# Order and engines of the head in a two-layer kernel of styled convolutions and feed-forward products

## The chip, the core and the metric

The kernel runs on one core of a Trainium2 chip. The core has TensorE (matrix products; PE in the profile, its weight loads PEld), VectorE (DVE), ScalarE (ACT), GpSimd (POOL) and SyncE (SP); each takes its instructions in the order in which they stand in its own queue, and waits for the others by semaphores. DMAs are issued from SP, ACT and POOL. The metric is the device time of one execution in microseconds (us).

## The reference, cut to what matters

Two layers run one after the other on x of 32 x 64 x 1024. Each is a chain of four small convolutions over 64 channels, scaled per sample by a style, and behind it a feed-forward product over the 1024 positions; the result is added to x. The head of the kernel is about the first part:

```python
def _layer(x, style, w, b, mw, mb, typ):
    s = style @ mw.T + mb
    weight = SCALE * w * s[:, None, :, None]
    demod = lax.rsqrt(jnp.sum(weight * weight, axis=(2, 3)) + EPS)
    weight = weight * demod[:, :, None, None]
    ...  # 'same', 'upsample' + blur, 'same', blur + 'downsample'; each + bias
x = x + _L0_ffn_ref(_L0_cond_ref(x, cond_512, ...), A, B, Wr)
x = x + _L1_ffn_ref(_L1_cond_ref(x, cond_512, ...), qweight, scales, zeros, bias)
```

The first feed-forward product picks 16 of 64 experts of rank 16 for each row; the second has weights of four bits.

## The kernel before, in words

All samples are worked on in 16 pairs: two samples' 64 channels fill the 128 partitions. The four convolutions are linear, so all but the first are composed into one set of filters per pair. For pair p of layer i:

- `load_x` (L523) fetches the samples into two buffers, `xdv(n % 2)`. A buffer is free again once `differences` (L538) has read it.
- `differences` scales by the style and forms three tiles (`xe`): one on ACT (L541), two on VectorE (L542, L543). `first` (L548) makes three products `c` with the matrix c0 (L554, L559) and adds bias and scale (ACT L556, VectorE L560 to L563).
- `composed1` (L460) makes the product `g` of w2t with scaled weights `r` (GpSimd L462), copied to `gs` by ACT (L476). `composed2` (L481) makes `f` from `gs` and the blurred weights w1b (18 passes on TensorE, L488), and copies it out (ACT L500, VectorE L501, GpSimd L503).
- `rest` (L566) applies the filters (`r`, L577), with ACT L590 and L585, GpSimd L586 and L587, VectorE L591. `outer` (L594) puts the four border columns in, which `ends` (L358) has computed apart; `turned` (L621) transposes the result for the feed-forward product (`h`, L662).

`factors` (L158) makes a layer's tables, in steps that a `yield` ends:

- step 1 issues the loads: mw (the style's weights), cwr, cur, biases; on SP and on ACT's queue;
- step 2 squares the weights (L192 to L195), spreads them into cw, cu, c0 and w3 (ACT L199, L203, L204; GpSimd L200), builds the blurred weights in six sums and two copies (GpSimd L213, L218), transposes the third convolution's weights into w2t (TensorE L223, ACT L224), multiplies the style (`sps`, L230), adds mb (L233), squares (L236), multiplies by the squared weights (`dps`, L239), takes root and reciprocal (ACT L247, VectorE L248);
- step 3 makes the scales `al` and biases `be` and their copies by pairs, alp, bep, styp (L256 to L275);
- step 4 carries the biases through the convolutions, two products `cs` (L282), each behind the other's result, to cst and cst2 (L284 to L286), which L590 reads.

`ends` works on the border columns of all pairs at once, in a chain: `ye` (L391), scaled; `ue` (L410), scaled; a blur; `ve` (L435), scaled; a blur; `re` (L446), scaled; copies into `re` (L455). "Scaled" is a product on VectorE (L371) and a sum on GpSimd (L372). A blur is two sums on GpSimd (L419, L420) and one instruction on VectorE (L421).

PSUM tiles come from three rings: mps has one bank (all of `sps`, `dps`, `cs`, `g`, `f`, `ye`, `ue`, `ve`, `re`, and w2t's transposes), cps three (`c`, `r`, transposes), fps four. A tile of a ring waits for the readers of the one whose bank it takes.

The order on each engine is made by a scheduling layer from the program's order and its own estimate of times; `tc.issue_after(v)` holds what is issued inside it behind instruction v in that order. It sets where an instruction stands in its queue and is no wait on the chip. `done` remembers such instructions by name.

The head of the main program, L898 to L930, runs step 1, loads pair 0, runs steps 2 and 3, begins pair 0 (`begin`: differences, first, composed1), runs step 4, loads pair 1, makes pair 0's filters (`weights(0)`), issues eight DMAs of the first product's weights from GpSimd (`load_a`, L304), begins pair 1, and interleaves `ends` with `rest` of pair 0. Behind it the main loop starts: `split_weights` (L290) divides each block of those weights into parts (VectorE L143, L299; ACT L298; GpSimd L297), held behind the last copy of `re`, `outer` and `turned`. The second layer's `factors` (set1, L977) runs a step at a time between pairs of the first layer's second product (`o`, L662, with transposes `ht`, L756), near 500 us.

Of the kernel before, what the change touches and what calls it, by code (L numbers as in the profile page):

```python
# [61 lines left out]
def adaln_ffn_kernel(ctx: ExitStack, tc: tile.TileContext, t, out: bass.AP):  # L62
# [95 lines left out]
    def factors(i, *rooms):  # L158
# [35 lines left out]
        for h in range(2):  # L194
            nc.vector.tensor_tensor(wsq[:, :, h], sq[:, :, 0], sq[:, :, 2], ALU.add)  # L195
# [5 lines left out]
        for h, hs in enumerate(halves):  # L201
            for e, o, k in (((0, 0, 0), (2, 0, 2), (2, 1, 1)), ((0, 0, 1), (0, 1, 0), (2, 1, 2)))[h]:
                nc.scalar.copy(c0[hs, e, halves[o]], cwr[hs, 0, k])  # L203
        nc.scalar.copy(w3, cwr[:, 3])  # L204


        t0 = tmp(NB + 1, C)
        t1 = tmp(NB + 1, C)
        nc.gpsimd.memset(t0.rearrange("p a b -> p (a b)"), 0.0)
        nc.gpsimd.memset(t1.rearrange("p a b -> p (a b)"), 0.0)  # L210
        nc.gpsimd.tensor_copy(t0[:, 1 : 1 + KT], cwr[:, 1])
        for n in range(KT + 1, NB + 1):
            nc.gpsimd.tensor_tensor(  # L213
                t1[:, 1 : 1 + n], t0[:, 1 : 1 + n], t0[:, 0:n], ALU.add
            )
            t0, t1 = t1, t0
        for hs in halves:
            done["blur"] = nc.gpsimd.tensor_copy(w1b[hs, :, hs], t0[hs, 1 : 1 + NB])  # L218


        ps = mpst(f"w2t{i}")
        for k in range(KT):
            nc.tensor.transpose(ps[:, k * P : (k + 1) * P], cw[:, 2, k], ident)  # L223
        nc.scalar.copy(w2t.rearrange("p a b -> p (a b)"), ps[:, : KT * P])  # L224
# [8 lines left out]
        nc.vector.tensor_tensor(sty, spv, mb.unsqueeze(2).to_broadcast([P, NL, B]), ALU.add)  # L233
        nc.vector.tensor_copy(sty0, sty[:, 0])

        nc.vector.tensor_tensor(sty2, sty, sty, ALU.mult)  # L236
        dpv = mpst(f"dps{i}")[:, : NL * B].rearrange("p (a b) -> p a b", b=B)
# [9 lines left out]
        nc.scalar.activation(dem, dpv, AF.Sqrt, bias=eps, scale=0.5)  # L247
        nc.vector.reciprocal(dem, dem)  # L248
# [109 lines left out]
    def ends(i, lo, hi, room, behind=None):  # L358
        n = hi - lo
        g = f"{i}_{lo}"  # L360
        used = [0]
# [6 lines left out]
        def scaled(dst, ps, l):  # L368
            a = alp[:, l, lo:hi].unsqueeze(2).to_broadcast([P, n, dst.shape[2]])
            b = bep[:, l, lo:hi].unsqueeze(2).to_broadcast([P, n, dst.shape[2]])  # L370
            nc.vector.tensor_tensor(dst, ps, a, ALU.mult)  # L371
            nc.gpsimd.tensor_tensor(dst, dst, b, ALU.add)  # L372
# [8 lines left out]
        with tc.issue_after(behind.ins) if behind else nullcontext():  # L381
            nc.vector.tensor_tensor(xe[:, :, 1:7], xg[:, lo:hi, 0, 0:6], s, ALU.mult)
            nc.vector.tensor_tensor(xe[:, :, 7:13], xg[:, lo:hi, 1, 2:8], s, ALU.mult)
# [32 lines left out]
        def blur(dst, v, count):  # L416

            m = sides(tmp(2 * count))
            nc.gpsimd.tensor_tensor(dst, v[..., 0:count], v[..., 3 : 3 + count], ALU.add)  # L419
            nc.gpsimd.tensor_tensor(m, v[..., 1 : 1 + count], v[..., 2 : 2 + count], ALU.add)  # L420
            nc.vector.scalar_tensor_tensor(dst, m, 3.0, dst, ALU.mult, ALU.add)  # L421
# [16 lines left out]
        scaled(ve[:, :, 2:14], ps, 2)  # L438
# [12 lines left out]
        scaled(rp, ps, 3)  # L451
# [96 lines left out]
    def first(i, n, xe):  # L548
# [8 lines left out]
        for q, w_, d in ((0, HQ, y[:, 0, :HQ]), (2, HQ - 1, y[:, 1, 1:HQ])):  # L557
            ps = cpst(f"c{i}_{n}_{q}")[:, :w_]
            nc.tensor.matmul(ps, c0[:, q], xe[:, q, :w_], start=True, stop=True)  # L559
            nc.vector.scalar_tensor_tensor(d, ps, a, yt[:, :w_], ALU.mult, ALU.add)  # L560
# [5 lines left out]
    def rest(i, n, y, f):  # L566
# [7 lines left out]
        for q, (m0, m1, n_) in enumerate(((0, 2, w_), (1, 3, HQ), (4, 5, w_))):  # L574
# [9 lines left out]
            if q == 1:  # L584
                nc.scalar.activation(m[:, q, :n_], ps, AF.Copy, scale=a)  # L585
                nc.gpsimd.tensor_tensor(u, m[:, 0, :w_], m[:, 1, :w_], ALU.add)  # L586
                nc.gpsimd.tensor_tensor(r[:, 1], m[:, 0, :w_], m[:, 1, 1:HQ], ALU.add)  # L587
            else:
                b = (cst if q == 0 else cst2)[:, n : n + 1]
                nc.scalar.activation(m[:, q, :n_], ps, AF.Identity, bias=b, scale=a)  # L590
        nc.vector.tensor_tensor(r[:, 0], m[:, 2, :w_], u, ALU.subtract)  # L591
# [320 lines left out]
    run(set0)  # L912
    first_done = done["xe"]
    load(1)
    weights(0)
    with tc.issue_after(done["sum"].ins):
# [162 lines left out]
```

## Time and profile before

Three runs gave 1017.24, 1017.95 and 1020.43 us, median 1017.95. One other execution was profiled: 1017.49 us, of which the span in the profile is 1015.4.

| | PE | PEld | DVE | ACT | POOL |
|---|---|---|---|---|---|
| busy us of the span | 953.8 | 841.4 | 634.7 | 368.6 | 466.9 |
| 0 to 25 us | 10.41 | 8.47 | 14.13 | 9.37 | 16.05 |
| 25 to 50 us | 18.52 | 15.17 | 13.45 | 8.79 | 13.83 |
| 50 to 75 us | 21.84 | 17.34 | 13.12 | 8.20 | 12.86 |
| 100 to 125 us | 24.08 | 17.63 | 9.57 | 9.14 | 10.83 |
| 175 to 200 us | 24.86 | 23.57 | 15.43 | 10.65 | 10.20 |

Busy time is the time with at least one instruction of the engine under way. Lines of the chain of waits give start, duration, engine, tile and source line; the chain is followed back from the last instruction, at each step to what released it. An fp32 product is recorded as two passes per instruction, so "x18" are nine products. PEclk is the TensorE clock that was granted, in tenths of full speed.

### The profile page before, as it was taken

To read this page: it belongs to the slowest core of one execution; us is meant where nothing else is said; L and a number is where in the kernel's file an instruction comes from. 1 tells how busy PE (TensorE), PEld (TensorE's weight loads), DVE (VectorE), ACT (ScalarE), POOL (GpSimd) and SP (SyncE) were. 2 spreads that over 40 slices of the span, in tenths; PEclk is the share of its full clock that TensorE was granted. 3 is DMA by queue.
4 is the path that set the end of the run, shared out by engine and by line. 5 is a ranking of instruction groups with operands and counts; after the bars stand their busy time and mean duration, and the time that the engine had idled before them with its cause. 6 is when DMAs were issued, how large, how long until landed. Compare 5 with 4: busy or idle time off the path is not lost.

```text
span 1015.4 us, 14211 instructions
## 1 busy us (share of the span) xinstructions
PE 953.8 (94%) x5046; PEld 841.4 (83%) x5046; DVE 634.7 (63%) x1275; ACT 368.6 (36%) x693; POOL 466.9 (46%) x638
## 2 busy tenths in 40 slices
PE   4788889999999999999989998999899999999997
PEld 3666679999999999994668887888898999899986
DVE  5557366666666666346974554486667766776654
ACT  3335344444444444323321111163334333433331
POOL 6557454443444334435762223226545555555544
PEclk9979989999999999999999999999999999999999
DMA  4631122222222221242353333352112221222111
GB/s 99 183 118 42 42 63 63 63 63 63 63 63 76 71 63 65 81 146 98 98 181 131 125 125 125 104 152 98 63 63 87 92 71 63 85 88 78 42 63 42
DMA packets 39894, 88.83 MB, mean 87 GB/s; under 512 B 12080, under 2 KB 20528, under 8 KB 39824
## 3 DMA queue, kind: packets, MB, share of 16 engines
q1 hardware_dynamic: 37616, 82.48, 25.9%
q0 software_dynamic: 1248, 4.46, 1.4%
q10 hardware_dynamic: 960, 0.99, 0.4%
q8 instruction: 40, 0.66, 0.3%
q14 instruction: 30, 0.25, 0.1%
HBM read 62.74 MB, written 25.17 MB: 87 GB/s over the span
## 4 chain that ended last, share of the span: by engine, by line
PE 74%; DVE 9%; POOL 6%; issue 5%; ACT 5%; DMA 1%; POOLq 0%; ACTq 0%; DVEq 0%; SPq 0%
PE h L662 17%; PE r L577 15%; PE o L662 13%; PE q L840 11%; PE f L488 8%; PE c L559 5%; DVE h L143 2%; PE c L554 2%; ACT yt L556 1%; ACT thx L604 1%; POOL wa L297 1%; PE ht L756 1%; DVE cv L563 1%; DVE sc L854 1%; DVE hs L684 1%
## 5 line engine op out<-in xcount | busy, mean ns | idle before, releaser
L577 PE MATMUL r<-cv 128*128 128x256 f32 (+1 forms) x768 | 181.6, 383 | 5.1 <-ACT rt L590 4.6
L577 PEld LDWEIGHTS r<-cv 128*128 128x128 f32 x768 | 143.2, 190 | 28.2 <-ACT rt L590 5.8
L590 ACT ACTIVATE rt<-r,cst,al 128x256 f32<-128x256 f32 x128 | 72.4, 565 | 164.2 <-PE r L577 151.8
L591 DVE TENSOR_TENSOR rs<-rt,ru 128x256 f32<-128x256 f32 x64 | 43.0, 672 | 103.4 <-ACT rt L590 55.5
L488 PEld LDWEIGHTS f<-gs,w1b 128*128 128x128 f32 x576 | 90.5, 200 | 3.8 <-ACT gs L476 1.1
L488 PE MATMUL f<-gs,w1b 128*128 128x192 f32 (+1 forms) x576 | 91.5, 315 | 1.2 <-ACT gs L476 0.6
L503 POOL TENSOR_TENSOR cv<-cv 128x256 f32<-128x256 f32 x64 | 48.0, 751 | 82.0 <-DVE cv L501 71.8
L501 DVE COPY cv<-f 64x448 f32<-64x448 f32 x64 | 39.9, 624 | 68.6 <-ACT cv L500 68.5
L586 POOL TENSOR_TENSOR ru<-rt 128x256 f32<-128x256 f32 x64 | 42.0, 656 | 86.4 <-ACT rt L585 86.4
L840 PE MATMUL q<-wq,thx 128*128 128x342 f32 x384 | 79.9, 345 | 1.6 <-ACT thx L604 1.6
L559 PE MATMUL c<-cv,c 128*128 128x257 f32 (+1 forms) x256 | 72.7, 406 | 8.8 <-ACT yt L556 5.5
L855 POOL TENSOR_TENSOR o<-o,sc 128x342 f32<-128x342 f32 (+1 forms) x48 | 42.0, 875 | 70.0 <-DVE o L852 62.0
L662 PE MATMUL h<-wa,thx 128*128 128x352 f32 (+1 forms) x336 | 70.7, 345 | 3.0 <-ACT thx L604 3.0
L500 ACT COPY cv<-f 64x448 f32<-64x448 f32 x64 | 33.9, 530 | 96.6 <-PE f L488 75.6
L840 PE MATMUL q<-wq,tlx 128*128 128x342 f32 x384 | 68.2, 320 | 0.0
L559 PEld LDWEIGHTS c<-cv,c 128*128 128x128 f32 x256 | 46.5, 195 | 25.3 <-ACT yt L556 16.9
L840 PEld LDWEIGHTS q<-wq,thx 128*128 128x128 f32 x384 | 62.7, 189 | 3.8 <-ACT thx L604 1.7
L662 PE MATMUL h<-wa,tdx 128*128 128x352 f32 (+1 forms) x336 | 64.3, 334 | 0.0
L662 PE MATMUL o<-wb,thh 128*128 128x512 f32 x224 | 61.1, 403 | 2.0 <-DVE cv L792 2.0
L543 DVE SCALAR_TENSOR_TENSOR cv<-cv,sty 128x256 f32<-128x256 f32 x64 | 62.7, 980 | 0.5
L560 DVE SCALAR_TENSOR_TENSOR cv<-c,al,yt 128x257 f32<-128x257 f32 (+1 forms) x128 | 57.1, 478 | 9.1 <-PE c L559 5.1
L662 PE MATMUL h<-wa,tlx 128*128 128x352 f32 (+1 forms) x336 | 62.0, 326 | 0.0
(252 smaller groups left out, 1943.2 us busy)
## 6 DMA issues: line engine op xcount, KB each, us to landing
cv<-in_x_dram SPq DMA_DIRECT2D x64, 256.0 KB, 4.0
hgd<-hs SPq DMA_DIRECT2D x16, 512.0 KB, 2.6
hg<-hgd SPq DMA_DIRECT2D x16, 512.0 KB, 3.7
x1d<-x SPq DMA_DIRECT2D x16, 512.0 KB, 2.9
cv<-x1d SPq DMA_DIRECT2D x128, 64.0 KB, 2.3
xb<-x1d SPq DMA_DIRECT2D x16, 512.0 KB, 3.3
out_dram<-o SPq DMA_DIRECT2D x16, 512.0 KB, 2.6
cv<-in_x_dram SPq DMA_DIRECT2D x13, 512.0 KB, 4.3
```

What stands on the lines that cost most here:

```text
L488: done["f"] = nc.tensor.matmul(ps[:, j * C : (j + rhs.shape[1]) * C].rearrange("p (a b) -> p a b", b=C), w1b[:, NB - 1 - q], rhs, start=(n ...
L503: done["sum"] = nc.gpsimd.tensor_tensor(f[:, 4 * P :].rearrange("p (a b) -> p a b", b=P), v[:, :, 0], v[:, :, 1], ALU.add)
L543: done["xe"] = nc.vector.scalar_tensor_tensor(xe[:, 2, : HQ - 1], behind, s, xe[:, 1, : HQ - 1], ALU.mult, ALU.subtract)
L559: nc.tensor.matmul(ps, c0[:, q], xe[:, q, :w_], start=True, stop=True)
L560: nc.vector.scalar_tensor_tensor(d, ps, a, yt[:, :w_], ALU.mult, ALU.add)
L577: nc.tensor.matmul(ps, f[:, k * P : (k + 1) * P], y[:, q, j : j + n_], start=(j == 0), stop=(j == 1),)
L586: nc.gpsimd.tensor_tensor(u, m[:, 0, :w_], m[:, 1, :w_], ALU.add)
L590: nc.scalar.activation(m[:, q, :n_], ps, AF.Identity, bias=b, scale=a)
L591: nc.vector.tensor_tensor(r[:, 0], m[:, 2, :w_], u, ALU.subtract)
L662: nc.tensor.matmul(banks[l == 2], toks[key][l][:, k], w[:, cols], start=(k == 0 and l != 1), stop=(k == NC - 1 and l in (2, min(n, 2) - 1)),)
L840: nc.tensor.matmul(ps, half[:, k], wq[at(k)][:, c * QC : (c + 1) * QC], start=(k == 0 and j == 0), stop=(k == NC - 1 and j == 1),)
L855: nc.gpsimd.tensor_tensor(o[:, cs], o[:, cs], s, ALU.add)
```

## The change

- In `factors`, the style product, its sum, sty0 and the square stand right behind the copies of the weights, ahead of the blur; the sum is held behind the last squared weights (`made`). The transposes into w2t come last, behind `dps`; they use the ring cps instead of mps, and their copy on ACT is held behind the root. The root is held behind the last c0 copy, the reciprocal behind the fourth of the six blur sums.
- For layer 0 the six blur sums run on VectorE instead of GpSimd; so do the sums of `scaled` and of the blur in `ends`. Layer 1 keeps GpSimd.
- `ends` takes a list of instructions, one for each of three places (xe, the scaling of `ve`, the scaling of `re`), to stand behind: pair 0's differences, and the last VectorE instruction of `rest` of its two samples.
- Step 4 yields between its two products. In the head, the first part runs behind `weights(0)`'s products, the second behind pair 1's last `c`; set1 takes one step more.
- `outer` of pair 0 is held behind its last GpSimd sum in `rest`; `weights(1)` behind the last `re` copy, `outer` and the last ACT instruction of `rest`.

In the order of the engines this gives, in the head: TensorE `sps`, `dps`, `w2t`, `c`, `g`, `f`, `c` with `cs`, `g`, `r` with `cs`, `ye`, `r`, `ue`, `r`, `ve`, `re`, `f`. VectorE gains six blur sums between L246 and the copies of step 3, and eight sums in `ends`; the differences of sample 5 (pair 2) stand between the scaling of `ye` and that of `ue`. On ACT the copy into w2t stands behind the root. GpSimd loses the same fourteen sums. SP's order differs only near 510 us, in loads for the second layer. In the second layer's set, TensorE has `sps`, `w2t`, `ht`, three `o` passes and `dps`, where it had `w2t`, five `ht` passes, `sps`, `ht`, six `o` passes and `dps`; its second `cs` moves one pair later.

```diff
+        sty2 = tmp(NL, B)
+        spv = mpst(f"sps{i}")[:, : NL * B].rearrange("p (a b) -> p a b", b=B)
+        for l in range(NL):
+            nc.tensor.matmul(
+                spv[:, l], mw[:, l].rearrange("p a b -> p (a b)"), condT, start=True, stop=True
+            )
+        with tc.issue_after(made.ins):
+            nc.vector.tensor_tensor(sty, spv, mb.unsqueeze(2).to_broadcast([P, NL, B]), ALU.add)
+        nc.vector.tensor_copy(sty0, sty[:, 0])
+        nc.vector.tensor_tensor(sty2, sty, sty, ALU.mult)
+        eng = nc.vector if i == 0 else nc.gpsimd
...
-            nc.gpsimd.tensor_tensor(
-                t1[:, 1 : 1 + n], t0[:, 1 : 1 + n], t0[:, 0:n], ALU.add
-            )
+            v = eng.tensor_tensor(t1[:, 1 : 1 + n], t0[:, 1 : 1 + n], t0[:, 0:n], ALU.add)
+            if n == NB - 2:
+                blurred = v
...
-        ps = mpst(f"w2t{i}")
-        for k in range(KT):
-            nc.tensor.transpose(ps[:, k * P : (k + 1) * P], cw[:, 2, k], ident)
-        nc.scalar.copy(w2t.rearrange("p a b -> p (a b)"), ps[:, : KT * P])
...
-        nc.scalar.activation(dem, dpv, AF.Sqrt, bias=eps, scale=0.5)
-        nc.vector.reciprocal(dem, dem)
+        with tc.issue_after(copied.ins):
+            root = nc.scalar.activation(dem, dpv, AF.Sqrt, bias=eps, scale=0.5)
+        with tc.issue_after(blurred.ins):
+            nc.vector.reciprocal(dem, dem)
+        ps = cpst(f"w2t{i}")
+        for k in range(KT):
+            nc.tensor.transpose(ps[:, k * P : (k + 1) * P], cw[:, 2, k], ident)
+        with tc.issue_after(root.ins):
+            nc.scalar.copy(w2t.rearrange("p a b -> p (a b)"), ps[:, : KT * P])
         yield
...
             nc.vector.tensor_tensor(dst, dst, be[:, l], ALU.add)
+            if l == 2:
+                yield
...
             nc.vector.tensor_tensor(dst, ps, a, ALU.mult)
-            nc.gpsimd.tensor_tensor(dst, dst, b, ALU.add)
+            eng.tensor_tensor(dst, dst, b, ALU.add)
...
-            nc.gpsimd.tensor_tensor(dst, v[..., 0:count], v[..., 3 : 3 + count], ALU.add)
-            nc.gpsimd.tensor_tensor(m, v[..., 1 : 1 + count], v[..., 2 : 2 + count], ALU.add)
+            eng.tensor_tensor(dst, v[..., 0:count], v[..., 3 : 3 + count], ALU.add)
+            eng.tensor_tensor(m, v[..., 1 : 1 + count], v[..., 2 : 2 + count], ALU.add)
...
-        scaled(ve[:, :, 2:14], ps, 2)
+        with next_behind():
+            scaled(ve[:, :, 2:14], ps, 2)
...
-        scaled(rp, ps, 3)
+        with next_behind():
+            scaled(rp, ps, 3)
...
-    run(set0)
-    first_done = done["xe"]
+    anchors = [done["xe"]]
     load(1)
     weights(0)
+    with tc.issue_after(done["f"].ins):
+        next(set0)
     with tc.issue_after(done["sum"].ins):
         araw = load_a()
     with tc.issue_after(done["f"].ins):
         begin(1)
-    set_ends = ends(0, 0, NP, block(2, [P, 3 * AW], F32, "room2"), first_done)
+    with tc.issue_after(done["c"].ins):
+        run(set0)
+    set_ends = ends(0, 0, NP, block(2, [P, 3 * AW], F32, "room2"), anchors)
     for h in range(2):
         next(set_ends)
         later(0, h, whole=False)
+        anchors.append(done["r0"])
     run(set_ends)
-    for h in range(2):
-        outer(h, rs[0][h])
+    with tc.issue_after(done["r"].ins):
+        for h in range(2):
+            outer(h, rs[0][h])
     load(2)
-    weights(1)
+    with ExitStack() as stack:
+        for v in ("re", "outer", "m"):
+            stack.enter_context(tc.issue_after(done[v].ins))
+        weights(1)
```

More of the change, by code (lines that the diff above doesn't have):

```diff
@@ L194, in factors @@
         for h in range(2):
-            nc.vector.tensor_tensor(wsq[:, :, h], sq[:, :, 0], sq[:, :, 2], ALU.add)
+            made = nc.vector.tensor_tensor(wsq[:, :, h], sq[:, :, 0], sq[:, :, 2], ALU.add)
         for hs in halves:
@@ L202, in factors @@
             for e, o, k in (((0, 0, 0), (2, 0, 2), (2, 1, 1)), ((0, 0, 1), (0, 1, 0), (2, 1, 2)))[h]:
-                nc.scalar.copy(c0[hs, e, halves[o]], cwr[hs, 0, k])
+                copied = nc.scalar.copy(c0[hs, e, halves[o]], cwr[hs, 0, k])
         nc.scalar.copy(w3, cwr[:, 3])
+        sty2 = tmp(NL, B)
[9 more added lines that the diff above has]
+        eng = nc.vector if i == 0 else nc.gpsimd
         t0 = tmp(NB + 1, C)
@@ L218, in factors @@
             done["blur"] = nc.gpsimd.tensor_copy(w1b[hs, :, hs], t0[hs, 1 : 1 + NB])
-        ps = mpst(f"w2t{i}")
-        for k in range(KT):
-            nc.tensor.transpose(ps[:, k * P : (k + 1) * P], cw[:, 2, k], ident)
-        nc.scalar.copy(w2t.rearrange("p a b -> p (a b)"), ps[:, : KT * P])
-        sty2 = tmp(NL, B)
-        spv = mpst(f"sps{i}")[:, : NL * B].rearrange("p (a b) -> p a b", b=B)
-        for l in range(NL):
-            nc.tensor.matmul(
-                spv[:, l], mw[:, l].rearrange("p a b -> p (a b)"), condT, start=True, stop=True
-            )
-        nc.vector.tensor_tensor(sty, spv, mb.unsqueeze(2).to_broadcast([P, NL, B]), ALU.add)
-        nc.vector.tensor_copy(sty0, sty[:, 0])
-        nc.vector.tensor_tensor(sty2, sty, sty, ALU.mult)
         dpv = mpst(f"dps{i}")[:, : NL * B].rearrange("p (a b) -> p a b", b=B)
@@ L355, in unpacked, with ends @@
         return wq, aux
-    def ends(i, lo, hi, room, behind=None):
+    def ends(i, lo, hi, room, behind=()):
         n = hi - lo
         g = f"{i}_{lo}"
+        eng = nc.vector if i == 0 else nc.gpsimd
         used = [0]
@@ L380, in ends, with next_behind @@
         s = styp[:, lo:hi].unsqueeze(2).to_broadcast([P, n, 6])
-        with tc.issue_after(behind.ins) if behind else nullcontext():
+        behind = iter(behind)
+        def next_behind():
+            v = next(behind, None)
+            return tc.issue_after(v.ins) if v else nullcontext()
+        with next_behind():
             nc.vector.tensor_tensor(xe[:, :, 1:7], xg[:, lo:hi, 0, 0:6], s, ALU.mult)
@@ L450, in ends @@
         rp = tmp(4)
-        scaled(rp, ps, 3)
+        with next_behind():
+            scaled(rp, ps, 3)
         dst = re[:, 2 * lo : 2 * hi].rearrange("p (n two) s -> p n two s", two=2)
@@ L558, in first @@
             ps = cpst(f"c{i}_{n}_{q}")[:, :w_]
-            nc.tensor.matmul(ps, c0[:, q], xe[:, q, :w_], start=True, stop=True)
+            done["c"] = nc.tensor.matmul(ps, c0[:, q], xe[:, q, :w_], start=True, stop=True)
             nc.vector.scalar_tensor_tensor(d, ps, a, yt[:, :w_], ALU.mult, ALU.add)
@@ L586, in rest @@
                 nc.gpsimd.tensor_tensor(u, m[:, 0, :w_], m[:, 1, :w_], ALU.add)
-                nc.gpsimd.tensor_tensor(r[:, 1], m[:, 0, :w_], m[:, 1, 1:HQ], ALU.add)
+                done["r"] = nc.gpsimd.tensor_tensor(r[:, 1], m[:, 0, :w_], m[:, 1, 1:HQ], ALU.add)
             else:
                 b = (cst if q == 0 else cst2)[:, n : n + 1]
-                nc.scalar.activation(m[:, q, :n_], ps, AF.Identity, bias=b, scale=a)
-        nc.vector.tensor_tensor(r[:, 0], m[:, 2, :w_], u, ALU.subtract)
+                done["m"] = nc.scalar.activation(m[:, q, :n_], ps, AF.Identity, bias=b, scale=a)
+        done["r0"] = nc.vector.tensor_tensor(r[:, 0], m[:, 2, :w_], u, ALU.subtract)
         return r
```

## The prediction

> **What bounds the kernel now.** First the page's 40 slices: TensorE is the engine with the most work, and it has holes only in the first four slices (25.4 us each). After that its row reads 8 or 9 throughout.
>
> ```profile
> PE   4788889999999999999989998999899999999997
> PEclk9979989999999999999999999999999999999999
> ...
> PE 74%; DVE 9%; POOL 6%; issue 5%; ACT 5%; DMA 1%; POOLq 0%; ACTq 0%; DVEq 0%; SPq 0%
> ```
>
> So the end is set by TensorE's work plus the time for which it stands still at the start. The build order of both kernels is the same on TensorE but for the head (up to the second `f` product) and a few places near 500 us, so only these two stretches are worked out. The chain of waits in order of time (start, duration, what) shows what the head waits for:
>
> ```profile
> 8.16 0.89 PE w2t L223 x3
> 9.07 0.49 ACT w2t L224
> 9.60 1.93 PE sps L230 x8
> 11.55 0.30 DVE room L233
> 12.86 1.14 DVE c L246
> 14.10 1.18 DVE room L262
> 15.47 1.28 DVE styp L272
> 16.78 0.96 DVE room L248
> ...
> 29.34 4.17 PE f L488 x18
> ...
> 47.86 0.82 POOL room L372
> 48.75 0.56 POOL room L419
> 49.32 0.53 POOL room L420
> 49.87 0.40 DVE room L421
> 50.41 2.27 PE ve L435 x6
> ...
> 56.93 5.28 PE f L488 x18
> ```
>
> To be seen: the style product (`sps`) stands behind the transposes and their copy; three small VectorE instructions take over 1.1 us each; the end columns pass between VectorE and GpSimd before `ve`. TensorE's own waits up to 57 us are 8.2 before `w2t`, 4.4 before the first `c`, 5.3 before `ve`, 2.4 before `re`. The second `f` (56.93) is my gauge: behind it both kernels run the same orders on all engines, and the weights' splitting, which the chain follows next, starts right beside it (VectorE L143 at 58.09, after the last `re` copy). A shift of this `f` is a shift of the end.
>
> **Part 1, style product first.** `sps` needs the two mw transfers: the second is issued at 2.53 and the pair takes 3.5 us at the median, so it is there at 6.3. `sps` lasts 1.93, to 8.2. The sum on it (L233) is put behind L195 on VectorE, which ends at 9.05: **9.1 instead of 11.55**. L233, L234, L236 take 0.3+0.2+0.3 (L234's 0.79 was beside a GpSimd sum; a like copy, L266, took 0.33), so `dps` starts at 10.0 (13.01 before) and ends after 1.89 at 11.9. ACT has done its c0 copies (1.08) and the table load (1.28) by 10.8; the root (0.37) ends at 12.3. The transposes follow at 11.9 to 12.8, their copy ends 13.25, and the first reader of w2t, `g`, comes after 20: hidden.
>
> **Part 2, blur on VectorE.** GpSimd's six sums (0.73 to 1.41 each, last one ending at 16.72) become six on VectorE. From its rows (256 elements 0.41, 768 elements 0.96) the sizes 256 to 576 cost 0.41, 0.48, 0.55, 0.62, 0.68, 0.75 = 3.5 us, in series with the tables. What goes is the stretching: L246 took 1.21 here and 0.27 in the second layer's set, L262 1.25 against 0.18, L272 1.45 for two against 0.16 each, about 3.2 us. VectorE then: L261, L262, L264, L272 to 10.4, L246 to 10.65, four sums with hand-offs to 12.8, reciprocal 0.96 to 13.8, sum five, al0 and be0's factors to 14.7, sum six to 15.45, the remaining copies 1.0 to 16.45. The copies into w1b (1.36) and `r` (1.10) follow on GpSimd to 18.0; needed by `g` after 20. First difference on VectorE: **16.45 instead of 19.25**; ACT's half is earlier still (14.0 instead of 18.47), so the first `c` product (cold, 1.23) is out of the way. The five `c` products behind it and `g` took 5.67 without a gap (20.49 to 26.16): now 17.1 to 22.8. `gs` 0.54: 23.3.
>
> **Part 3, bias terms in two parts.** Before, `cs` twice with its VectorE steps stood between `gs` and `f`: 26.73 to 29.34 = 2.6 us. Now `f` follows `gs`: **23.3 instead of 29.34**. At 4.17 it ends at 27.5 (33.51 before). The cost comes later, partly on the path: `cs` 2 waits for the bank of `f` and for VectorE's second copy out of it, and `g` of pair 1 waits for `cs` 2's scaling. With copies at 0.53/0.63 and differences at 0.6 each, `c` of inputs 2 and 3 end at 31.7, `g` at 32.7, `cs` 3 at 33.8; its scaling stands behind two differences on VectorE, so `ye` starts at 35.0. Before: 39.35. Thus 1.7 of the 6.0 are given back here.
>
> **Part 4, end columns.** VectorE in place of GpSimd takes L372 out from behind the eight weight DMAs (38.12 to 43.53). A step costs 0.33 to 0.45 on VectorE by L371's sizes, 0.5 to 0.85 on GpSimd. `ye` scaled: 36.6, `ue` to 37.5. VectorE then has the differences of input 5 ahead of the scaling of `ue`. Their transfer is issued when its buffer is released, about 31.4, lands after 4.3 (the row of this transfer in that place) plus 0.7 while the weights' first packets join it: 36.4; ACT 0.7, VectorE 1.2: 38.3. Five steps (0.45, 0.45, 0.39, 0.39, 0.39 and hand-offs) to 40.4; and 0.5 for the GpSimd sums L586/L587 (0.64 each) that read beside them. `ve` at **40.9 instead of 50.41**. From there to the second `f` it was 6.52, with 2.43 between `ve` and `re`; VectorE alone needs 1.8: 5.9. Second `f` at **46.8 instead of 56.93: 10.1 us earlier**.
>
> Two transfers must follow. The weights' DMAs (issued from GpSimd behind the second L503) go out at 31.7 instead of 38.12; the last took 16.2 and landed at 59, so now near 52.5, where the first product that reads this block (69.8 before) is due at 59.7. Inputs 6 and 7 (10 to 11 us to landing in that crowd) land by 50 and are due at 56.
>
> **Part 5, second layer.** TensorE's order near 505 becomes `sps`, `w2t`, `ht`, three `o` passes, `dps`. The 0.66 wait of `sps` goes; `dps` still waits for VectorE's square, at 509.0 instead of 509.54, but with only three passes ahead of it: 2.4 idle in place of 0.66+1.34. A **loss of 0.4**. Cover gone, each us more on VectorE costs one. `cs` 3 one step later is long before its use: nothing.
>
> **Sum.** 10.1 − 0.4 = 9.7 off the profiled execution's 1017.5 (span 1015.4 and 2.1 around it): 1007.8. The median of the runs shown, 1017.95, lies 0.5 above that execution, well inside their spread of 3.2; I take **1007.7**.
>
> [...] TensorE's clock: the second `f` took 5.28 with 0.50 granted between 50 and 62 us, the same product 2.53 near 115 at 1.00; the first `f` was cold until 32 and took 4.17. [...] The changes at 28.7, 32.1, 49.2, 62.9, 83.3, 86.8 agree with one raster. [...] by the row 4.17. I take the row, since the 0.5 gap at `gs` follows and the clock did fall at 28.7 after gaps of 1.4. With all of `f`, `ve`, `re` and the second `f` warm the gain grows by 4 to 6; with `f` all cold it shrinks by 1.1.
>
> [...] VectorE is busier beside the eight issues now. The rows: 0.97 and 0.76 for a large pair beside VectorE work, 0.76 and 0.77 for the like pair without. By rows, 0.2; [...] 7 us of spare lie behind the last transfer. I take the rows.
>
> **Rivals.** (a) *Input 5 is caught behind the weights* (0.12). For: the next inputs took 10 to 11 us when they met those DMAs, and VectorE queues the end columns behind input 5's differences. Against: it is issued about 1 us before the large weight DMA. Price 10 less 5 us: 1013. (b) *The clock goes with the change* (0.18): 1003.5. (c) *Slower* (0.03): the root on ACT now holds w2t's copy and the next pair's casts behind `dps` in the second layer, where TensorE has no slack. The casts have to be done by 520 and need 3.6 us, so it decides once VectorE's square comes after 516, instead of 509; to eat the 9.7 as well and more than 3, it must come 20 us late: 1021. Nothing of that length stands ahead of it. (d) *The head doesn't set the end* (0.05): the splitting chain on GpSimd from 58 to 130 waits for something that doesn't move, and the result is 1016. Against: every input of it that I find moves along. My forecast has the remaining 0.62, with 1005 to 1011 as its own range.
>
> **Numbers.** From 1003.5 (clock) to 1013 (input 5). A difference of 0.3% (3 us) is about what this measurement tells from none: faster 0.93, same 0.04, slower 0.03.
>
> **What would show it.** `sps` near 6.3 and L233's like near 9.1; VectorE's short rows under 0.3 us before 12; first `f` within 1 us of 23.3 and straight behind `gs`; `ve` near 41 with no GpSimd step between `ue` and `re`; second `f` near 47; later waits of TensorE as before. Wrong if the second `f` moves and the end doesn't, if input 5's transfer takes over 7 us, or if TensorE idles over 3 us near 507.

## The result and the profile after

Six runs of the changed kernel have a median of 1006.45 us (1002.47 to 1010.68); six of the kernel before, beside them, 1017.34 (1014.90 to 1020.43). The ratio is 0.9895, with a 95% interval of 0.9863 to 0.9927: faster by 1.0%, 0.7 to 1.4. The profiled execution took 1006.92 us with a span of 1005.1, 10.3 less than the span before. A second set of six runs, below, gave 1010.10 (1005.32 to 1012.04; ratio 0.9930, 0.9909 to 0.9950). All twelve have a median of 1008.1. The changed kernel scatters over 9.6 us, and what this scatter is made of is a good part of what follows. "Cold" stands below for TensorE at a granted clock of 0.50, "warm" for 1.00.

First the page of the changed kernel: TensorE's busy share and its granted clock in 40 slices, and the shares of the chain of waits.

```profile
PE   4889799999999999989999998998899999999997
...
PEclk9999899999999999999999999998999999999999
...
PE 75%; DVE 9%; ACT 5%; issue 4%; POOL 4%; DMA 2%; ACTq 0%; POOLq 0%; DVEq 0%
```

TensorE's first four slices read 4, 8, 8, 9 instead of 4, 7, 8, 8, and GpSimd's share of the chain is 4% instead of 6%. The 7 in the fifth slice, with the clock's dip there, is the wait of 4.1 us that the kernel before has in its sixth (at 128.2; here at 115.1). The clock's dip in the third slice, at the end of the head, is gone. A new dip stands at the 28th slice, near 685 us. Then the chain of waits (start, duration, what), for comparison with the lines shown of before:

```profile
17.88 2.08 PE c L576 x4
...
23.34 0.54 ACT gs L493
23.87 0.04 issue
23.92 2.80 PE f L505 x18
...
36.66 1.09 DVE cv L559
37.75 0.85 DVE cv L560
38.60 0.37 DVE room L380
...
39.55 0.39 DVE room L434
...
40.82 1.23 PE ve L450 x6
...
44.41 0.88 PE re L462 x6
...
45.59 4.47 PE f L505 x18
```

The first `f` stands straight behind `gs` (23.92, before 29.34). Between `ue` and `ve` there is no GpSimd step any more. The end columns now wait for the two differences of input 5 (L559, L560: 1.09 and 0.85 us beside GpSimd's sums, where the same two took 0.7 each for input 4). `ve` starts at 40.82 instead of 50.41, and the second `f` at 45.59 instead of 56.93, which is 11.3 us earlier.

Followed to the end by VectorE's last step for r (`rs`) and the joins of the outputs, the lead over the kernel before is 13.1 us from 115 to 465 us, 14.4 from 520 to 610, 13.3 at 674 and 10.1 from 704 on.

### The profile page after: what moved, and what is told of

The parts are those of the page before. It is cut to its first block, busy times and chain, and to the rows that moved or that the text cites. A ratio compares the mean times of both kernels' runs of the same rounds, so it can differ in the third digit from the quotient of the medians.

```text
span 1005.1 us, 14223 instructions
## 1 busy us (share of the span) xinstructions
PE 951.8 (95%) x5046; PEld 840.1 (84%) x5046; DVE 636.0 (63%) x1289; ACT 367.6 (37%) x693; POOL 455.2 (45%) x624
## 3 DMA queue, kind: packets, MB, share of 16 engines
q0 software_dynamic: 1248, 4.46, 1.4%
## 4 chain that ended last, share of the span: by engine, by line
PE 75%; DVE 9%; ACT 5%; issue 4%; POOL 4%; DMA 2%; ACTq 0%; POOLq 0%; DVEq 0%
PE h L679 17%; PE r L594 16%; PE o L679 13%; PE q L857 12%; PE f L505 8%; PE c L576 6%; DVE h L143 2%; PE c L571 2%; ACT yt L573 1%; ACT thx L621 1%; POOL wa L305 1%; PE ht L773 1%; DVE sc L871 1%; DVE hs L701 1%; ACT wq L358 1%
## 5 line engine op out<-in xcount | busy, mean ns | idle before, releaser
L505 PEld LDWEIGHTS f<-gs,w1b 128*128 128x128 f32 x576 | 88.2, 195 | 4.3 <-ACT gs L493 2.0
L505 PE MATMUL f<-gs,w1b 128*128 128x192 f32 (+1 forms) x576 | 89.0, 310 | 1.6 <-ACT gs L493 1.2
L576 PEld LDWEIGHTS c<-cv,c 128*128 128x128 f32 x256 | 46.8, 196 | 28.1 <-ACT yt L573 16.8
L560 DVE SCALAR_TENSOR_TENSOR cv<-cv,sty 128x256 f32<-128x256 f32 x64 | 65.1, 1019 | 0.5
```

The lines of the kernel that those rows point to most:

```text
L505: done["f"] = nc.tensor.matmul(ps[:, j * C : (j + rhs.shape[1]) * C].rearrange("p (a b) -> p a b", b=C), w1b[:, NB - 1 - q], rhs, start=(n ...
L560: done["xe"] = nc.vector.scalar_tensor_tensor(xe[:, 2, : HQ - 1], behind, s, xe[:, 1, : HQ - 1], ALU.mult, ALU.subtract)
L576: done["c"] = nc.tensor.matmul(ps, c0[:, q], xe[:, q, :w_], start=True, stop=True)
```

## The experiments

All kernels below are the changed kernel with the edit that is shown. Starts are in us from the profiled execution of each; "lead" is how much earlier than in the kernel before the 22nd `rs` starts (321.03 there); the last column is the median of the timed runs, their spread and number.

| kernel | first f | ye | ve | second f | lead | span | runs |
|---|---|---|---|---|---|---|---|
| before | 29.34 | 39.2 | 50.41 | 56.93 | | 1015.4 | 1016.8 (1011.6 to 1020.7, 57) |
| changed | 23.92 | 34.88 | 40.82 | 45.59 | 13.1 | 1005.1 | 1006.45 (1002.5 to 1010.7, 6) |
| r_after | 24.32 | 35.28 | 41.24 | 46.01 | 12.4 | 1005.2 | 1010.10 (1005.3 to 1012.0, 6) |
| m_style | 27.00 | 37.96 | 43.91 | 48.68 | 9.7 | 1008.8 | 1011.03 (1009.4 to 1013.9, 6) |
| m_blur | 25.74 | 36.70 | 42.65 | 47.42 | 12.0 | 1001.0 | 1006.94 (1002.8 to 1011.5, 6) |
| m_cs | 26.84 | 36.84 | 43.52 | 48.93 | 8.9 | 1009.6 | 1010.97 (1003.2 to 1012.0, 7) |
| m_ends | 24.60 | 35.57 | 45.15 | 51.67 | 7.8 | 1006.7 | 1013.34 (1008.5 to 1016.7, 22) |
| l1_old | 24.22 | 35.55 | 43.96 | 49.38 | 9.2 | 1009.7 | 1008.93 (1005.3 to 1011.5, 6) |
| v9 | 24.61 | 35.96 | 42.00 | 46.60 | 11.9 | 1006.6 | 1007.42 (1002.5 to 1008.5, 6) |
| v13 | 22.27 | 28.56 | 38.88 | 44.77 | 13.9 | 1004.1 | 1006.54 (1003.8 to 1008.7, 6) |
| guard | 23.85 | 35.19 | 41.26 | 46.03 | 11.5 | 1004.7 | 1005.14 (1002.3 to 1006.5, 4) |
| guard_again | 23.66 | 35.01 | 40.89 | 45.66 | 11.6 | 1001.6 | 1006.33 (1003.4 to 1008.2, 4) |
| guard_l1_old | 23.30 | 34.62 | 40.70 | 45.51 | 12.2 | 1004.1 | 1006.29 (1004.9 to 1006.7, 4) |
| head2 | 23.91 | 31.84 | 40.38 | 45.30 | 14.1 | 1002.4 | 1005.50 (1003.7 to 1008.6, 6) |

Since the times scatter, the parts are read from the starts, and against the mean of the two traces of the changed kernel (first f 24.1, ye 35.1, ve 41.0, second f 45.8, lead 12.8).

### The changed kernel once more: r_after

> The changed kernel once more, for a second trace of it. Theory (the granted clock of TensorE steps down and up by itself, and where a step falls is not set by the kernel): all starts up to the second f agree with the first trace within 0.5 us as long as the clock is the same (dps 10.5, first f 23.9, ve 40.8, second f 45.6), but the two places where the first trace was at 0.50 (45.9 to 49.3 and 681 to 688) move or go, and the span differs by up to 4 us with them. Rival (the loss of 4 us near 680, where the lead on the kernel before shrank from 14.4 to 10.1 us, is made by the change): the products c and g behind 680 are cold again at 2.1 and 1.5 us, and the span is within 1 us of 1005.1.

Here the head agrees within 0.5 us (the `c` and `g` products ahead of the first `f` stayed slow for longer: the last `c` pair takes 1.06 us, in the first trace 0.59; the clock's row shows 1.00 there in both, so this slow start is read from the durations alone), and the cold stretches lie at the same places, the one behind 680 us too. The span differs by 0.1. So this run speaks for the rival; the pair guard and guard_again below speaks against it.

### Each part taken back by itself

The style product behind w2t again (first layer only), m_style:

```diff
-        sty2 = tmp(NL, B)
-        spv = mpst(f"sps{i}")[:, : NL * B].rearrange("p (a b) -> p a b", b=B)
...
         eng = nc.vector if i == 0 else nc.gpsimd
...
+        ps = mpst(f"w2t{i}")
+        for k in range(KT):
+            nc.tensor.transpose(ps[:, k * P : (k + 1) * P], cw[:, 2, k], ident)
+        nc.scalar.copy(w2t.rearrange("p a b -> p (a b)"), ps[:, : KT * P])
+        sty2 = tmp(NL, B)
+        spv = mpst(f"sps{i}")[:, : NL * B].rearrange("p (a b) -> p a b", b=B)
...
```

> The changed kernel with the first layer's style product back behind the transposes of w2t and their copy. Theory (the parts lie in series on the path, part 1 of the prediction): the sum on sps comes at 11.6 instead of 9.2, dps at 13.0 instead of 10.5, the reciprocal at 15.4 instead of 13.0, the first difference on VectorE at 19.5, the first f at 26.3, the second f at 48.0 and the end 2.4 us later. Rival (the blur's sums on VectorE fill the wait, and the style is not what ends last): the blur's sums move ahead and the first f comes within 0.8 us of 23.9.

Measured: the sum on `sps` at 11.71, `dps` at 12.55, reciprocal 15.33, first difference 19.50, and second `f` 48.68. That is 2.9 us later, and the lead is 3.1 us smaller. The part is in series with the rest, as the prediction had it.

The blur sums on GpSimd again, m_blur:

```diff
-        eng = nc.vector if i == 0 else nc.gpsimd
+        eng = nc.gpsimd
         t0 = tmp(NB + 1, C)
```

> The changed kernel with the first layer's six blur sums back on GpSimd. Theory (what VectorE gains by not being stretched it pays back as 3.5 us of sums in series, so this part alone is worth about nothing): VectorE's short rows between 9.5 and 13 are stretched to about 1 us again, the first f comes within 0.8 us of 23.9, second f and end within 1 us. Rival A (the stretching was the larger part): first f and end 1.5 to 3 us later. Rival B (the series of sums is the larger part): first difference on VectorE at 15.5 to 16.0 instead of 17.2, first f and end 1 us earlier or more.

VectorE's timeline in this kernel (start, duration, line and operation):

```profile
9.94 1.64 DVE L278 COPY styp<-room 64x16 f32<-64x16 f32 x2
...
12.38 0.95 DVE L247 RECIPROCAL room<-room 128x128 f32<-128x128 f32 x1 [0.48 <-ACT room L245]
...
15.30 1.57 DVE L275 COPY bep<-room 64x64 f32<-64x64 f32 x2
```

The two styp copies take 1.64 us where the changed kernel shows 0.34, and the bep copies 1.57 instead of 0.76. The stretching comes back. First and second `f` are 1.6 us later: rival A, just. It didn't reach the end: the second `f` was warm here (2.78 us instead of 4.46) and no cold stretch lay near 680. This kernel has 17 us of half clock within its span, the changed one 31, and the shortest span of all.

The bias terms in one piece ahead of `f`, m_cs:

```diff
+    run(set0)
     load(1)
     weights(0)
-    with tc.issue_after(done["f"].ins):
-        next(set0)
...
-    with tc.issue_after(done["c"].ins):
-        run(set0)
```

> The changed kernel with the first layer's bias terms in one piece ahead of the first f. Theory (part 3 of the prediction: 2.6 us ahead of f, of which 1.7 come back later): first f at 26.5 to 26.9 instead of 23.9, ye at about 35.8 instead of 34.9, second f at about 46.5 and the end 0.9 us later. Rival A (nothing is given back): ye, second f and end 2.6 us later. Rival B (the bias terms are hidden behind the inputs' transfers either way): ye, second f and end within 0.3 us.

TensorE's timeline in m_cs; the bracket holds the idle time before a row and what ended it:

```profile
24.33 0.85 PE L288 MATMUL cs<-room,cw 128*128 128x32 f32 x6 [0.62 <-ACT gs L493]
25.70 0.85 PE L288 MATMUL cs<-room,cw 128*128 128x32 f32 x6 [0.51 <-DVE room L291]
26.84 4.32 PE L505 MATMUL f<-gs,w1b 128*128 128x192 f32 x18 [0.28 <-DVE cst L290]
...
47.10 1.51 PE L462 MATMUL re<-room,cw 128*128 128x64 f32 x6 [2.38 <-DVE room L436]
```

The first `f` comes 2.7 us later, as expected. But of these only 0.9 are back at `ye`; `ve` is 2.5 later, the second `f` 3.1, and the lead 3.9 smaller. That is worse than rival A. Part of it is clock: with two small `cs` products and three waits just ahead of it, `f` runs cold (4.32 us; 2.78 in each of the twelve traces where it stands straight behind `gs`, and 4.17 in the kernel before, at a mean granted clock of 0.66, which has `cs` there too), and so does `re` (1.51 instead of 0.86).

The end columns' sums on GpSimd again, m_ends:

```diff
         g = f"{i}_{lo}"
-        eng = nc.vector if i == 0 else nc.gpsimd
+        eng = nc.gpsimd
```

> The changed kernel with the end columns' bias sums and blur sums back on GpSimd (their places in the order kept). Theory (part 4 of the prediction: GpSimd's steps stand behind the eight weight DMAs and are longer): ye stays at about 34.9, its sum with bep waits for the DMA issues' end at 36.7, ve comes at 44 to 46 instead of 40.8, the second f at 49 to 52.5 and the end by the head 3.5 to 7 us later. Rival (with the first f early the DMA issues are over before the sums are due, so the engine hardly matters): ve and the second f at most 1.5 us later.

GpSimd's timeline in m_ends:

```profile
37.37 0.76 POOL L381 TENSOR_TENSOR room<-room,bep 128x160 f32<-128x160 f32 x1
...
42.56 0.86 POOL L381 TENSOR_TENSOR room<-room,bep 128x288 f32<-128x288 f32 x1
43.50 0.56 POOL L434 TENSOR_TENSOR room<-room 128x224 f32<-128x224 f32 x1
44.02 0.56 POOL L435 TENSOR_TENSOR room<-room 128x224 f32<-128x224 f32 x1
```

The last weight DMA is issued until 37.35, and `ye`'s sum follows it without a gap. `ue`'s sum then stands behind the sums for r, until 42.56, on an engine that the changed kernel doesn't ask. `ve` at 45.15 and the second `f` at 51.67 (5.9 later), the lead 5.0 smaller: the theory, in the middle of its range. The rival's DMA issues were not over before the first sum was due. Of the 5.9 us, 4.1 stand at `ve`; the other 1.7 are clock, since `ve` (2.26) and `re` (1.51) ran cold.

The four losses of lead are 3.1, 0.7, 3.9 and 5.0: together 12.7, as much as the whole lead. That the sum comes out so closely is partly luck: two traces of the changed kernel differ by 0.7, and the losses of m_cs and m_ends hold the cold products named above. The medians of the timed runs, against 1008.1 of the changed kernel's twelve, lie 2.9 (m_style), 2.9 (m_cs) and 5.2 us (m_ends) higher, m_blur's 1.2 lower. The issue orders of `outer` and `weights(1)` were not taken back, and what they are worth by themselves is not known.

### The second layer alone: l1_old

The branches of m_style for the second layer instead of the first, and no issue order for its root.

> The changed kernel with only the second layer's factors in the old order (transposes of w2t and their copy ahead of the style product, no issue orders). The first 440 us agree with the changed kernel. Theory of the prediction (part 5: the new order costs 0.4 us there): from 530 to 610 us this kernel is 0.4 us ahead of the changed one. Rival A (the trace of the changed kernel shows a gain there): 1.3 us behind it from 530 on, with TensorE waiting near 507 before sps and before dps as in the kernel before. Rival B (the difference there is only where a cold stretch of TensorE falls): within 0.3 us, once both have one stretch of 3.4 us there.

Two things happened. In the second layer the lead stays at 9.2 us from 465 to 560 us, where the changed kernel gains 1.3 (13.1 to 14.4; 12.4 to 13.7 in r_after). Each has one cold stretch of 3.4 us there (514 to 517 in this kernel, 496 to 501 in the two traces of the changed one). TensorE's waits in the changed kernel (the last row of each view is cut off by the end of its window):

```profile
490.64 0.97 PE L210 MATMUL sps<-condT,cv 128*128 128x32 f32 x8
...
495.39 1.05 PE L236 MATMUL dps<-cv 128*128 128x32 f32 x8 [1.84 <-DVE cv L217]
...
510.35 0.93 PE L679 MATMUL o<-wb,thh 128*128 128x512 f32 x3 [1.11 <-DVE cv L809]
```

and in l1_old:

```profile
496.19 1.08 PE L244 MATMUL sps<-condT,cv 128*128 128x32 f32 x8 [0.61 <-ACT w2t L239]
...
500.35 1.05 PE L253 MATMUL dps<-cv 128*128 128x32 f32 x8 [1.32 <-DVE cv L250]
...
513.94 1.55 PE L697 MATMUL o<-wb,thh 128*128 128x512 f32 x3 [2.04 <-DVE cv L827]
```

The waits before `dps` are nearly the same in sum (1.93 against 1.84). What is gained is in the next wait for VectorE, 2.04 against 1.11, some 15 us later. That speaks for rival A, with a place that no theory had named.

The other thing was in the head, where this kernel has the changed kernel's order on every engine: `ve` came at 43.96, 2.7 us later than in r_after. The timelines of both show why. First r_after:

```profile
30.49 0.68 DVE L560 SCALAR_TENSOR_TENSOR cv<-cv,sty 128x256 f32<-128x256 f32 x1
30.54 1.17 POOL L520 TENSOR_TENSOR cv<-cv 128x256 f32<-128x256 f32 x1 [1.41 <-DVE cv L518]
...
31.80 0.55 SPq L546 DMA_DIRECT2D cv<-in_x_dram  x1
...
32.63 0.76 POOL L322 DMA_DIRECT2D araw<-in_aT_dram  x1
...
36.11 0.76 ACT L558 ACTIVATE cv<-cv,sty 128x257 f32<-128x257 f32 x1
```

And l1_old:

```profile
30.39 1.17 DVE L578 SCALAR_TENSOR_TENSOR cv<-cv,sty 128x256 f32<-128x256 f32 x1
30.44 0.73 POOL L538 TENSOR_TENSOR cv<-cv 128x256 f32<-128x256 f32 x1 [1.41 <-DVE cv L536]
...
32.08 0.76 POOL L340 DMA_DIRECT2D araw<-in_aT_dram  x1
32.19 0.55 SPq L564 DMA_DIRECT2D cv<-in_x_dram  x1
...
39.67 0.76 ACT L576 ACTIVATE cv<-cv,sty 128x257 f32<-128x257 f32 x1 [3.31 <-DMA cv<-in_x_dram]
```

VectorE's last difference of input 3 and GpSimd's sum for `f` run side by side, and one of the two is stretched to 1.17 us. Where it is GpSimd's, input 5's second transfer is issued (SPq) ahead of the first large weight DMA and has landed by 36.1. Where it is VectorE's, it goes out behind it and lands at 39.6. This is the prediction's rival (a). The order of the instructions does not decide it, since it is the same in both kernels; that it is decided anew in each execution is not shown, since the two traces of the changed kernel agree with each other.

### Moving input 5 and the end columns: v9, v13

v9 puts the differences of input 5 on VectorE behind the end columns' first blur:

```diff
-            xs = [differences(2 * p + h, *v) for h, v in enumerate(xin.pop(k))]
+            xs = []
+            for h, v in enumerate(xin.pop(k)):
+                with tc.issue_after(done["ze"].ins) if (k, h) == (2, 1) else nullcontext():
+                    xs.append(differences(2 * p + h, *v))
```

> The changed kernel with the two differences of input 5 on VectorE ordered behind the end columns' first blur (they stood ahead of the scaling of ue, 36.7 to 38.6). Theory (they hold the end columns up by what is left of them when ue is ready, about 0.6 to 1 us): ve at 39.9 to 40.2 instead of 40.8, the second f 0.6 to 1 us earlier, later products as before. Rival (the scaling then meets GpSimd's sums for r, and the input buffer's later release costs more): ve within 0.3 us, or c of input 5 and the following transfers later and the end not earlier.

`ve` came at 42.00: a miss. From `ue` to `ve` it took 3.44 us, against 3.98 in r_after, so the step itself is worth 0.5. But `ye` was 0.7 later in this execution, and its sum took 1.08 us instead of 0.46 (beside GpSimd's sums for r), so that `ue` was 1.3 later. The input was late as well (38.6 on ScalarE).

v13 has three moves; the third, not shown, orders input 5's differences behind cst2. `differ(0)` makes the differences of inputs 0 and 1:

```diff
-    for _ in range(2):
-        next(set0)
+    next(set0)
+    xes[0] = differ(0)
+    next(set0)
...
     weights(0)
+    set_ends = ends(0, 0, NP, block(2, [P, 3 * AW], F32, "room2"), anchors)
+    next(set_ends)
+    next(set_ends)
...
```

> The changed kernel with three further moves in the head: the differences of inputs 0 and 1 traced ahead of the tables, the end columns' ye and ue traced ahead of the second pair's inputs, and input 5's differences behind the second bias term. Theory (the head's chain still sets the end, us for us): first f at 22.4 to 23.0 instead of 23.9, ue at 31 to 32 instead of 36.9, ve at 35 to 37 instead of 40.8, second f at 42 to 43.5 instead of 45.6, and rs between 100 and 440 us earlier by the same 2 to 3.5 us; the end too, but for what cold stretches of TensorE add or take. Rival (with the end columns early the second f waits for r's scaling and the weights' splitting for its DMAs): second f not before 45, or the lead gone at 75 us.

The first `f` (22.27) and `ue` (31.60) came as the theory has them, and `ve` didn't. ScalarE's timeline shows what took it back:

```profile
36.53 0.75 ACT L558 ACTIVATE cv<-cv,sty 128x257 f32<-128x257 f32 x1 [2.98 <-DMA cv<-in_x_dram]
37.18 0.51 ACT L493 ACTIVATE gs<-g,alp 128x320 f32<-128x320 f32 x1
```

`gs` of the second pair is queued behind input 5, whose transfer again met the weights (issued at 30.3, landed at 36.4). The third bias term waits for the bank of `g` behind it. Of the 5.5 us by which `ue` was earlier, 1.1 is left in the lead.

### Input 5 ahead of the weights: guard, guard_again

One instruction more, a copy of one column on GpSimd that can't run before VectorE has released input 5's buffer:

```diff
-    with tc.issue_after(done["sum"].ins):
-        araw = load_a()
     with tc.issue_after(done["f"].ins):
         begin(1)
+    gd = tiny.tile([P, 1], F32, tag="gd", name="gd")
+    with tc.issue_after(done["sum"].ins):
+        seen = nc.gpsimd.tensor_copy(gd, xev(3)[:, 2, 0:1])
+    with tc.issue_after(seen.ins):
+        araw = load_a()
```

> The changed kernel with one more instruction: GpSimd copies one column of input 3's second difference into a scratch tile, and the eight weight DMAs are ordered behind that copy. So they cannot be issued before VectorE has released input 5's buffer. Theory (rival (a) of the prediction comes and goes: VectorE's difference of input 3 and GpSimd's sum for f stretch each other, and whichever is stretched decides whether input 5's transfer or the weights are issued first): in every execution input 5 is on ScalarE by 36.6, ve at 40.7 to 41.5, second f at 45.5 to 46.5, rs from 100 to 440 us as in the first two traces of the changed kernel (12.4 to 13.1 us ahead of the kernel before), and the slowest timed runs go. Rival (the landing at 38.6 and 39.7 in two traces was contention that this order does not set): input 5 on ScalarE after 38 again.

The trace of guard is a case where VectorE is the one that is stretched, as it is in the three other traces with this copy:

```profile
30.02 1.18 DVE L560 SCALAR_TENSOR_TENSOR cv<-cv,sty 128x256 f32<-128x256 f32 x1
...
31.83 0.55 SPq L546 DMA_DIRECT2D cv<-in_x_dram  x1
32.35 0.76 POOL L322 DMA_DIRECT2D araw<-in_aT_dram  x1
...
36.69 0.77 ACT L558 ACTIVATE cv<-cv,sty 128x257 f32<-128x257 f32 x1 [0.69 <-ACT rt L602]
```

All the same input 5 goes ahead of the first large weight DMA (L322), and ScalarE has it at 36.7, after at most 0.7 us of waiting. `ve` and the second `f` are those of r_after. The lead was a miss: 11.5, where 12.4 to 13.1 were expected. TensorE was cold for 6.8 us from 69.6 on, where the changed kernel's trace has 3.4; guard_again shows the same, and why is not known.

> The kernel of the run guard once more. Theory (input 5's place ahead of the weights is now fixed, and what is left of the spread is TensorE's cold stretches): input 5 on ScalarE by 36.8, ve at 40.5 to 41.5, no timed run above 1009, and the times fall on one line over the mean granted clock, about 0.8 us for each 0.001. Rival (the good times of the first four were luck): runs of 1010 and more come back, as in 5 of the 12 runs of the changed kernel.

Input 5 was on ScalarE at 36.4, and no run was above 1008.2. Both sets together: eight runs, median 1005.6, 1002.3 to 1008.2, where the changed kernel's twelve lie from 1002.5 to 1012.0 with six above 1009 and four at 1010 or more (the expectation above counts 1009.86 with them). Over the mean granted clock of each run the eight lie on a line of 0.77 us for each 0.001, with 0.6 us left over; the changed kernel's twelve have 1.7 left over. At a clock of 0.983 the line of the twelve stands at 1008.2, that of the eight at 1006.5. A late input in part of the twelve would do that, but neither of the two traces of the changed kernel shows one. The ratios to the kernel before, 0.9879 (0.9857 to 0.9901) and 0.9907 (0.9890 to 0.9924), don't stand apart from the changed kernel's, so guard scatters less, and is not shown to be faster.

This pair also bears on the clock. TensorE in guard, and then in guard_again, near 680 us, each behind the GpSimd sum that it waits for:

```profile
675.52 2.87 POOL L847 TENSOR_TENSOR o<-xb,aux 128x1024 f32<-128x1024 f32 x1 [1.21 <-DMA xb<-x1d]
...
680.23 0.94 PE L649 MATMUL t<-ident,rs 128*128 128x128 f32 x4 [2.38 <-POOL rs L613]
680.97 1.06 PE L571 MATMUL c<-cv,c 128*128 128x257 f32 x2
682.69 2.08 PE L576 MATMUL c<-cv,c 128*128 128x257 f32 x4 [0.66 <-ACT yt L573]
```

```profile
674.82 2.87 POOL L847 TENSOR_TENSOR o<-xb,aux 128x1024 f32<-128x1024 f32 x1 [0.55 <-DMA xb<-x1d]
...
679.53 0.74 PE L649 MATMUL t<-ident,rs 128*128 128x128 f32 x4 [1.73 <-POOL rs L613]
680.12 0.60 PE L571 MATMUL c<-cv,c 128*128 128x257 f32 x2
681.37 1.13 PE L576 MATMUL c<-cv,c 128*128 128x257 f32 x4 [0.66 <-ACT yt L573]
```

It is the same kernel, and at 673 us the two stand within 0.1 us. In guard a transfer (xb) then lands later, GpSimd's sum waits 1.21 us for it instead of 0.55, and TensorE behind it 2.38 instead of 1.73. There the clock goes to 0.50 for 6.8 us, and the lead falls from 13.8 to 10.5. In guard_again it stays at 1.00, and 13.7 stay to the end. The length of the wait alone doesn't decide, though: in v9 a cold stretch began at 682.4 behind a wait of 1.29. So a loss of 3 us near 680 us comes and goes in one and the same kernel, and the one that the changed kernel shows can't be put down to the change. Of the 14 traces, ten have cold stretches between 676 and 724 us; the kernel before, of which there is one trace, is one of the four without. Whether the change makes them more frequent is not shown.

### Second layer without the late input: guard_l1_old

> The kernel of the run guard with the second layer's factors in the old order. Theory (the new order of the second layer is worth 1.3 us, with TensorE's waits of 0.6 before sps and 1.3 before dps and 2.0 before the next o gone for 1.8 and 1.1): head and rs to 440 us within 0.5 us of the run guard, then 1.2 to 1.5 us behind it from 535 to 610 us. Rival (prediction, part 5): 0.4 us ahead of it there.

Missed: from 465 to 560 us this kernel's lead grows by 1.6 us, guard's by 1.3. The old order had no cold stretch here. It had one in the two other traces of the old order (3.4 us each), while all eleven traces of the new order have one between 492 and 508. With a stretch each, the new order is 1.3 ahead; the old one without is 0.3 ahead of the new one with. Whether the new order, with its 1.8 us of standstill, brings the stretch on each time, three traces against eleven don't decide.

### A further reordered head: head2

guard, with v13's differences, and the order second bias term, `ye`, third bias term, second pair's inputs, `ue`; input 5's differences behind the second blur and behind the last scaling of r.

> The changed kernel with the same guard and a reordered head: differences of inputs 0 and 1 traced ahead of the tables; second bias term, ye, third bias term and only then the second pair's inputs; ue ahead of the scaling of r; input 5's differences behind the end columns' second blur on VectorE and behind the last scaling of r on ScalarE. Theory (with input 5 out of the end columns' way the head is set by TensorE's own work): first f at 22.3, ue at 33.5 to 35, ve at 37.5 to 39, second f at 42 to 43.5, rs from 100 to 440 us 2 to 3 us ahead of the run guard. Rival (GpSimd's sums behind the DMA issues and ScalarE's scaling of r hold the second f now): second f not before 45.

The first `f` came at 23.91 and not at 22.3: the products ahead of it, in v13's order, were slow here (`g` 1.01 for two passes, 0.59 in v13; the granted clock is recorded as 1.00). `ue` stood behind the passes of r (36.56), and the second `f` came at 45.30: the rival. Its lead of 14.1 is the largest, with that `f` warm (2.78). 1005.50 us is no better than guard.

## Why the prediction was right, and where not

- **The sum.** Forecast 1007.7, measured 1006.45 in the six runs beside it and 1008.1 in all twelve. The mechanism held: the head set the end, and the lead of its last products was carried through. But that the number fits so well is luck, since the errors cancel: the head gave 3.0 more than 10.1, the second layer 1.7 more than −0.4, and then 1.1 went between 610 and 680 and 3.2 near 690. 9.7 + 3.0 + 1.7 − 1.1 − 3.2 = 10.1, about the 10.3 of the spans. Of the 3.0, 1.2 stand at the start of the second `f` (11.3 earlier instead of 10.1). The other 1.8 came behind it, 0.8 of them in that `f` (4.46 instead of 5.28), while the kernel before stayed cold until 62.9. So a shift of this `f` was not the whole shift of the end, as the prediction took it to be. Its reading that TensorE has holes only in the first four slices passes over the waits of 3.1 and 4.2 us at 82.8 and 128.2; they moved along unchanged (3.1 and 4.1), so nothing in the sum hung on it.
- **Part 1** held: `sps` 6.16, the sum on it 9.24 (9.1), `dps` 10.51 (10.0; the copy to sty0 still took 0.80 beside GpSimd's memsets). Taken back, it costs 2.9 where 2.4 were set.
- **Part 2** held in kind, with 17.16 for the first difference instead of 16.45: the bep and alp copies (0.76 and 0.91, where 1.0 was set for all the remaining copies) took about twice the 0.39 of before, beside GpSimd's copies into w1b. By itself the part is worth 1.6 at the second `f`. (In the second layer's set only one of the two L272 copies takes 0.16, the other 0.97; the changed kernel's two, 0.34 together, bear the prediction's figure out.)
- **Part 3**: the first `f` at 23.92 (23.3) was right, straight behind `gs`, and `ye` at 34.88 too (35.0). The mis-sized term is `f` itself: 4.17 from the row, measured 2.78 in each of the twelve traces where it follows `gs`. Taking the row was the wrong choice: it is that of an `f` behind `cs`, with 0.50 granted from 28.8 to 32.2. That the gap at `gs` would bring the same was the author's estimate; the changed kernel's `f` stands behind a gap of 0.62 there, at a granted clock of 1.00. Against m_cs the split is worth 3.1 at the second `f`, where "2.6 less 1.7" had been set: what was called given back went to `ye` by 0.9 only.
- **Part 4** held: `ve` at 40.82 (40.9), second `f` 45.59 (46.8). Late there are now input 5's differences, as the prediction put it. Weight DMAs issued at 31.25 with the durations of before; the last landed at 54.7 (52.5). The step from `ve` to the second `f` took 4.77 (5.9), and this hides two errors. VectorE's steps between `ve` and `re` were set at 1.8, but TensorE waited 2.38 there, as it had before (2.44). What made up for it is clock, which the sum left as it was: `ve` 1.21 (before 2.26), `re` 0.86 (1.51), both cold before and warm now. Around the end of the head the kernel before is cold for 13.6 us (49.3 to 62.9), the changed one for 3.4 (45.9 to 49.3).
- **Part 5 failed** in its sign ("a loss of 0.4"; measured a gain of 1.3): TensorE's wait before `dps` was 1.84, where 2.4 had been set and the kernel before has 2.0 in two waits, so no loss; and the wait for VectorE behind it, which the sum didn't look at, fell from 2.02 to 1.11. The gain of 1.3 holds with one cold stretch on each side.
- **The rivals.** (a) was real: it came in three of the eight traces in which no dependency orders input 5 and the weights and the two meet (l1_old 39.7, v9 38.6, v13 36.5 with ScalarE waiting for it), and in l1_old it costs 2.7 us at `ve`, not 5. The two traces of the changed kernel itself don't show it. (b) was half of the truth: the clock did go with the change in the head, and in these two traces what the sum gained was lost again to stretches further on. Over all runs an estimate can be made. The mean granted clock of the 57 runs of the kernel before is 0.9803, that of the changed kernel's twelve 0.9833. At 0.73 us for each 0.001 (below) this is worth 2.2 of the 8.7 us between the medians, and 6.5 are left at equal clock. (c) and (d) didn't come.

## What to carry to other kernels

When TensorE sets the end, price a step in the head by what it hands on to the end of the head and not by its own wait; leave-one-out runs read at fixed marks in the trace (a product's start, the lead over a long quiet stretch) separate parts of 1 us that timed runs scattering by 10 us can't. Where two transfers of different urgency are released by two engines within 1 us of each other, fix their order by a dependency: with one small copy ahead of the weights, input 5 was ahead of the first large one in all four traces. And before a gain or a loss far from the change is explained, take a second trace: here 6.8 us at half clock undid 3.3 us, a quarter of the lead, in one of two traces of the same kernel.

## What the runs showed of the hardware

- Every cold stretch of TensorE in the 14 traces lasts 3.4 us or a multiple of it (6.8 at 680.8 in the changed kernel, 13.6 at 49.3 in the kernel before), but for what the end of the trace cuts. In each trace all cold stretches begin on one raster of 3.413 us (in the kernel before at 28.8 and 6, 16, 29, 127 and 145 steps later; in the changed kernel at 45.9 and 7, 20, 118, 132, 167 and 186 steps later), and the raster lies differently from trace to trace (the first stretch of guard_l1_old starts at 45.0). The mean granted clock of a run tells most of its time: 57 runs of the kernel before fall by 0.73 us for each 0.001.
- Two instructions of VectorE and GpSimd started 0.05 us apart, VectorE's first, in twelve traces: one of them took 1.16 to 1.18 us and the other 0.67 to 0.74. In five it was GpSimd's that was stretched (r_after among them), in seven VectorE's (l1_old and guard among them). So which of the two starts first, by the recorded starts, does not tell which is stretched.
- A 256 KB transfer (input 5's second) beside the first large weight DMA: issued 0.8 us ahead of it, it took 4.1 to 4.3 us to landing (five traces); 0.5 ahead, 4.7 to 5.5 (four, all with guard's copy); 0.1 behind, 7.4, 6.0 and 6.1 (l1_old, v9, v13).
